# Where GpSimd widens the second norm's deviations in a two-direction state-space layer

## The chip, the cores and the metric

The kernel is one program on one core of a Trainium2 chip. The metric is the time of one execution on the device, in microseconds (us). Four runs of the kernel before took 17284.53 to 17308.42 us, with a median of 17295.28 us. A separate execution was recorded by the hardware profiler. It took 17300.45 us, and its span, from the first recorded instruction to the last, is 17298.6 us. All durations below are from that one execution.

A core has five engines with queues of their own: TensorE (PE in the profile, with PEld for its weight loads), VectorE (DVE), ScalarE (ACT), GpSimd (POOL) and SyncE (SP), which here only issues transfers. Each engine runs its queue in order, and an instruction at the head of a queue that waits holds up all behind it.

## The reference

The input is x, 8 images of 64 channels of 128 x 128 points, in float32. Four layers are applied one after the other, each as x = x + layer(groupnorm(x)): a deformable convolution, a 3x3 convolution, a pair of state-space scans, and a block that compares neighbouring points. The change lies in the third. Cut to what matters:

```python
def _layer_norm(x, g, b):                    # over the 64 channels of a point
    mu = jnp.mean(x, axis=-1, keepdims=True)
    var = jnp.mean((x - mu) ** 2, axis=-1, keepdims=True)
    return (x - mu) * jax.lax.rsqrt(var + EPS) * g + b
def _s5_block(x, i, ...):
    fx = _layer_norm(x, ln1_g[i], ln1_b[i])
    h = _s5_scan(fx, ...)                    # a scan forwards and one backwards
    x = jax.nn.gelu(h) + fx
    fx2 = _layer_norm(x, ln2_g[i], ln2_b[i]) # the second norm
    return fx2 @ ff_enc[i].T @ ff_dec[i].T + fx2
...
y_h = _s5_block(rows of the image, 0, *blk)
y_v = _s5_block(columns of the image, 1, *blk)
y = jnp.concatenate([y_h, y_v], axis=1)
return jnp.einsum('bihw,oi->bohw', y, fusion_w) + fusion_b[None, :, None, None]
```

Each of the two directions (rows, columns) has a forward and a backward scan over 16384 points. The second norm needs, for each point, one factor 1/sqrt(var + EPS), by which all 64 channels of that point are multiplied.

## The kernel before

The 8 images are handled as 4 pairs. The two images of a pair stand on the 128 partitions, 64 channels each. The deformable convolution of all pairs comes first, up to about 12100 us of the span. Then `rest` (line 451) takes pair after pair through the other three layers. In `scan_layer` (line 891) a pair first goes through `first_norm`, beside which the backward scan of direction 0 runs; then `ahead` (line 1250) runs for direction 0 with the backward scan of direction 1 beside it (the generator `aside`), and then `ahead` for direction 1 with nothing beside it.

`ahead` works in 16 groups of 1024 points (a group is 4 points by 256 blocks, and two images). A turn g of its loop is written in this order:

1. `scan(0, g + 1)`: the states of the next group (PE line 1154, ACT 1159, two DVE scans at line 1161).
2. `outputs(g)`: two PSUM tiles `py` from eight matmul calls (line 1208), gelu on ACT (1210), and the addition of `fx` on DVE (1211), into `h`, in two halves.
3. `rebuilt(g + 1)`: the states of the next group are turned back. For the backward and then the forward scan: a matmul `zt` (line 1187), a multiplication on GpSimd into `x` (1191), one on DVE into `xt` (1192) and a subtraction on GpSimd (1193). The tile `xt` has one buffer, so the second DVE multiplication needs the first subtraction to have read it.
4. `add(g - 1)`: for each half e of the group before: `spread` widens its 8 factors per partition to 8 x 64 on GpSimd (tile `yb`, line 849), four PE transposes bring them to channels in PSUM (`rb`, 852), ACT copies that to `rs` (1235), eight matmul calls mix the channels into `pm` (1240), DVE multiplies `pm` by `rs` (1241) and adds the result to the image in two instructions (1245). Tiles `yb` and `rs` have one buffer each. `rb`, `pm` and the tile `qc` below share one PSUM tag of two buffers.
5. `inputs(g + 2)` and `drive(g + 2)`: the drive of a later group, with one addition on GpSimd (`u`, line 1146).
6. `deviation(g)`: for each half a centring matmul (`qc`, 1220), a square on ACT (1222) and four small matmuls (1224) that leave 16 variances per partition; then `rsqrt` (line 104), 15 small DVE instructions in a row (`ln_...` in the profile, lines 108 to 118).
7. One step of `aside`: for direction 0 a turn of the backward scan of direction 1, with one more `u` on GpSimd.

This written order is not the order of the queues. The framework's planner goes over the instructions with costs of its own for each. When an engine is free in its reckoning, it takes from those that are ready then, with a free buffer for what they write, the one that was written first. So the written order decides only between instructions that are ready at the same time, and each engine's queue is what the planner's reckoning made of it. In the trace the order of GpSimd in a repeated turn of direction 0 is `u`, `u`, `yb` of half 0, both multiplications into `x`, the first subtraction, `yb` of half 1, the second subtraction.

`first_norm` (line 855) uses `spread` too, four times for each of its eight steps, with the tags `yb` and `xt` in turn.

Of the kernel before, what the change touches and what calls it, by code (L numbers as in the profile page):

```python
# [9 lines left out]
F32 = mybir.dt.float32  # L10
# [6 lines left out]
P = 128  # L17
C = 64
# [18 lines left out]
EPS = 1e-5  # L37
# [3 lines left out]
class Net:  # L41
# [800 lines left out]
            at = first + 2 * q  # L842
            self.nc.tensor.matmul(pv[:, at : at + 2], lhsT=sq[:, q * P : (q + 1) * P], rhs=self.imgmean, start=True, stop=True)  # L843

    def spread(self, wp, ptag, y, tag, ytag="yb"):

        nc = self.nc
        yb = wp.tile([P, 8, C], F32, tag=ytag, name=f"{tag}_yb", bufs=1)
        nc.gpsimd.tensor_copy(yb, y.unsqueeze(2).to_broadcast([P, 8, C]))  # L849
        rb = self.ps.tile([P, CH], F32, tag=ptag, name=f"{tag}_rb")  # L850
        for q in range(4):
            nc.tensor.transpose(rb[:, q * P : (q + 1) * P], yb[:, 2 * q : 2 * q + 2].rearrange("p i c -> p (i c)"), self.ident)
        return rb

    def first_norm(self, wp, p, a, b, r, nb):


        nc = self.nc
        af, bf = a.rearrange("p h w -> p (h w)"), b.rearrange("p h w -> p (h w)")
        center = wp.tile([P, P], F32, tag="center_r", name=f"center_r{p}", bufs=1)  # L860
        nc.vector.tensor_scalar(center, self.center, r, None, ALU.mult)
        pn = self.ps1.tile([P, 1], F32, tag="small", name=f"cn{p}")
        nc.tensor.matmul(pn, lhsT=self.center, rhs=nb, start=True, stop=True)
        cn = wp.tile([P, 1], F32, tag="cn", name=f"cns{p}", bufs=1)
        nc.vector.tensor_copy(cn, pn)

        def scale(n, y):
            for m in range(4):
                s = slice((4 * n + m) * CH, (4 * n + m + 1) * CH)
                rb = self.spread(wp, "y", y[:, 8 * m : 8 * m + 8], f"l1_{p}_{n}_{m}", ("yb", "xt")[m % 2])  # L870
                nc.vector.tensor_mul(bf[:, s], bf[:, s], rb)

        late = None
        for n in range(NCH // 4 - 1, -1, -1):
            pv = self.ps1.tile([P, 32], F32, tag="small", name=f"l1v{p}_{n}")
            for m in range(4):
                s = slice((4 * n + m) * CH, (4 * n + m + 1) * CH)
                pc = self.ps.tile([P, CH], F32, tag="x", name=f"pc{p}_{n}_{m}")
                nc.tensor.matmul(pc, lhsT=center, rhs=af[:, s], start=True, stop=True)
                sq = wp.tile([P, CH], F32, tag=("sq", "rs")[m % 2], name=f"sq{p}_{n}_{m}", bufs=1)  # L880
                nc.scalar.activation(sq, pc, AF.Square, bias=cn)
                nc.scalar.activation(bf[:, s], pc, AF.Identity, bias=cn)
                self.variances(pv, 8 * m, sq)
            if late:
                scale(*late)
                yield
            late = n, self.rsqrt(self.small, pv, 32, EPS, "ln32")
        scale(*late)
        yield

# [209 lines left out]
class Scan:  # L1100
# [112 lines left out]

    def deviation(self, g, hs):

        nc, net, tag = self.nc, self.net, f"{self.p}_{self.d}_{g}"
        pv = net.ps1.tile([P, 2, 2, 2, 2], F32, tag="small", name=f"l2v{tag}")
        for h in range(2):
            pc = net.ps.tile([P, CH], F32, tag="x", name=f"qc{tag}_{h}")
            nc.tensor.matmul(pc, lhsT=net.center, rhs=hs[:, h], start=True, stop=True)  # L1220
            sq = self.wp.tile([P, CH], F32, tag="sq", name=f"qs{tag}_{h}", bufs=1)
            nc.scalar.activation(sq, pc, AF.Square)
            for q in range(4):
                nc.tensor.matmul(pv[:, h, :, q % 2, q // 2], lhsT=sq[:, q * P : (q + 1) * P], rhs=net.imgmean, start=True, stop=True)
        return net.rsqrt(net.small, pv.rearrange("p a e m i -> p (a e m i)"), 16, EPS, "ln16")

    def add(self, g, hs, y):

        nc, net = self.nc, self.net
        for e in range(2):  # L1230
            h = hs[:, e]
            tag = f"{self.p}_{self.d}_{g}_{e}"
            rb = net.spread(self.wp, "x", y[:, 8 * e : 8 * e + 8], tag)
            rs = self.wp.tile([P, CH], F32, tag="rs", name=f"rs{tag}", bufs=1)
            nc.scalar.copy(rs, rb)
            pm = net.ps.tile([P, CH], F32, tag="x", name=f"pm{tag}")
            for j in range(2):
                mix = self.outs[:, MIX + j * C : MIX + (j + 1) * C]
                for i in range(2):
                    nc.tensor.matmul(pm[i * C : (i + 1) * C, j * NB : (j + 1) * NB], lhsT=mix, rhs=h[:, i, :], start=True, stop=True)  # L1240
            nc.vector.tensor_mul(rs, pm, rs)
            rs = rs.rearrange("p (j o m) -> p j o m", j=2, m=self.INNER)
            for j in range(2):
                at = self.blocks(self.a, g)[:, 2 * e + j]
                nc.vector.scalar_tensor_tensor(at, at, self.w["bias"], rs[:, j], ALU.add, ALU.add)  # L1245
        if self.d:
            for h in range(2):
                nc.vector.bn_stats(self.st[:, 2 * g + h, :], self.a[:, 64 * h : 64 * h + 64, 8 * g : 8 * g + 8])
# [70 lines left out]
```

## Time and profile before

| what | value |
|---|---|
| median of four runs | 17295.28 us |
| the profiled execution, its span | 17300.45 us, 17298.6 us |
| busy over the span: PE, DVE, POOL, ACT | 68%, 68%, 60%, 17% |
| a repeated turn of `ahead`, direction 0 (12580.00 to 12603.20 us) | 23.20 us: PE busy 21.83, DVE 16.34, ACT 9.65, POOL 9.54 |
| a repeated turn of `ahead`, direction 1 (13030.00 to 13050.55 us) | 20.55 us: PE busy 18.58, DVE 15.09, POOL 7.76, ACT 6.61 |
| granted PE clock in both turns | 1.00 |
| `yb` copies of `ahead`: instructions, one alone | 256, about 0.61 us |
| `yb` copies of `first_norm`: instructions, mean | 128, 615 ns |

Shares over the whole span are of little use here, since the layers have different limits. The change is read from the repeated turns, in the timeline, where each line gives the start in us, the duration, the engine, the line of the code, the instruction with its output and inputs, and in brackets how long the engine stood idle before it and what released it.

### The profile page before, as it was taken

The numbers are of one execution on the slowest core, as the hardware profiler recorded it, in microseconds if no ns is written. First come the engines' busy times: TensorE is split into PE (matmuls) and PEld (weight loads), VectorE is DVE, ScalarE is ACT, GpSimd is POOL, SyncE is SP. The second block draws the span as 40 slices with busy tenths as digits, with TensorE's granted clock in tenths as the row PEclk, the third lists the DMA queues.
The fourth block names the chain that finished last, engine by engine and source line by source line (L and its number), as shares of the span: only waits on it lengthen the run. The fifth ranks groups of instructions, "written<-read, shape, count | busy, mean of one in ns | idle before, by whom it ended". The sixth has DMA issues, their size and how long they took to land. (4 is left out here: it accounts for less than half of the span.)

```text
span 17298.6 us, 123578 instructions
## 1 busy us (share of the span) xinstructions
PE 11837.9 (68%) x33912; PEld 4220.1 (24%) x33912; DVE 11800.9 (68%) x27470; ACT 2925.7 (17%) x4956; POOL 10371.0 (60%) x10492
## 2 busy tenths in 40 slices
PE   5766565656675656666665665643898898898897
PEld 1111111111111111111111111111443443443443
DVE  5777777777777777777777777776465565565565
ACT  1101111111110011111001010001332332332331
POOL 3777777777777777777777777776232232232231
PEclk8977787877887768788787787865999999899897
DMA  6334444444433344443333333334223323323322
GB/s 192 121 116 127 140 149 151 133 147 143 146 117 115 114 134 146 148 134 116 113 116 114 114 117 113 113 107 138 52 57 97 94 55 101 90 56 101 92 53 73
DMA packets 966439, 1969.78 MB, mean 114 GB/s; under 512 B 216301, under 2 KB 517749, under 8 KB 931957
## 3 DMA queue, kind: packets, MB, share of 16 engines
q0 software_dynamic: 442368, 1208.55, 23.6%
q1 hardware_dynamic: 514532, 715.93, 13.4%
q10 hardware_dynamic: 8848, 37.40, 0.6%
q8 instruction: 275, 4.51, 0.1%
q14 instruction: 416, 3.40, 0.1%
HBM read 1516.67 MB, written 276.67 MB: 104 GB/s over the span
## 5 line engine op out<-in xcount | busy, mean ns | idle before, releaser
L388 POOL DMA_INDIRECT g<-table,idx x9216 | 8936.2, 970 | 2813.4 <-issue 2619.7
L397 DVE TENSOR_TENSOR g<-g,wts 128x256 f32<-128x256 f32 x9216 | 3805.3, 419 | 3138.0 <-DMA g<-table,idx 3123.2
L398 DVE TENSOR_REDUCE sm<-g 128x64 f32<-128x256 f32 x9216 | 4985.1, 579 | 0.9 <-DVE pos L352 0.2
L322 PE MATMUL po<-xe,wt 128*54 128x512 f32 (+3 forms) x8384 | 4730.1, 676 | 43.9 <-ACT ob L332 42.0
L402 PE MATMUL sp<-ident,sm 128*128 128x128 f32 x4096 | 1522.4, 376 | 4148.5 <-DVE sm L398 4136.4
L402 PEld LDWEIGHTS sp<-ident,sm 128*128 128x128 f32 x4096 | 625.6, 155 | 6930.9 <-DVE sm L398 5026.9
L405 ACT COPY s<-sp 128x512 f32<-128x512 f32 x1024 | 599.9, 586 | 8565.8 <-PE sp L402 8565.8
L322 PEld LDWEIGHTS po<-xe,wt 128*54 128x54 f32 x8384 | 929.6, 140 | 1415.4 <-issue 1068.0
L1146 POOL TENSOR_TENSOR u<-u,vs 128x512 f32<-128x512 f32 x256 | 326.0, 1274 | 1344.8 <-DVE vs L1145 1081.1
L411 PE MATMUL yp<-s,wd 128*64 128x512 f32 (+1 forms) x2560 | 823.5, 664 | 12.6 <-ACT s L405 12.6
L571 PE MATMUL c<-room,l_w 128*64 128x508 f32 (+1 forms) x3072 | 717.9, 597 | 16.0 <-DMA room<-nx 8.7
L849 POOL COPY l_yb<-ln_y 128x512 f32<-128x512 f32 x128 | 76.5, 615 | 1036.0 <-PE l1v L843 668.3
L1127 ACT ACTIVATE fx<-room,ln_b,ln_g 128x512 f32<-128x512 f32 x512 | 642.8, 1291 | 91.1 <-DMA in<-fx 61.7
L404 PE MATMUL s<-ident,sm 128*64 128x128 f32 x1024 | 346.7, 339 | 356.1 <-DVE sm L398 330.5
L1138 PE MATMUL pv<-in,tabs 128*128 128x512 f32 x1024 | 543.4, 654 | 5.2 <-DVE xt L1192 5.2
L1208 PE MATMUL py<-in,outs 128*128 128x512 f32 x1024 | 532.0, 624 | 2.7 <-ACT h L1210 2.7
L1208 PE MATMUL py<-x,outs 128*128 128x512 f32 x1024 | 504.0, 604 | 5.7 <-POOL x L1193 5.4
L1161 DVE TENSOR_TENSOR_SCAN z<-tabs,z,u 128x256 f32<-128x256 f32 x512 | 401.9, 804 | 82.1 <-POOL u L1146 59.6
L406 ACT COPY s<-s 64x128 f32<-64x128 f32 x1024 | 264.6, 258 | 722.7 <-PE s L404 722.2
L1245 DVE SCALAR_TENSOR_TENSOR room<-room,bias,rs 128x256 f32<-128x256 f32 x512 | 375.2, 785 | 6.9
L1193 POOL TENSOR_TENSOR x<-x,xt 128x512 f32<-128x512 f32 x256 | 327.8, 1281 | 68.0 <-DVE xt L1192 60.9
L1192 DVE TENSOR_TENSOR xt<-zt,tabs 128x512 f32<-128x512 f32 x256 | 175.6, 686 | 266.0 <-POOL x L1193 254.6
(1431 smaller groups left out, 11149.9 us busy)
## 6 DMA issues: line engine op xcount, KB each, us to landing
g<-table,idx POOLq DMA_INDIRECT x9216, 2.7
table<-q SPq DMA_DIRECT2D x512, 256.0 KB
in<-fx SPq DMA_DIRECT2D x1024, 128.0 KB
xe<-in_x_dram SPq DMA_DIRECT2D x56, 1408.0 KB
xs<-in_x_dram SPq DMA_DIRECT2D x32, 1024.0 KB
xt<-in_x_dram SPq DMA_DIRECT2D x32, 1024.0 KB
y<-ys SPq DMA_DIRECT2D x128, 256.0 KB
room<-in_x_dram SPq DMA_DIRECT2D x32, 1024.0 KB
```

Source lines behind the costliest of these rows:

```text
L322: nc.tensor.matmul(po[:, r0:r1, c0:c1], lhsT=wt[:, t, :], rhs=xe[:, row + r0 : row + r1, c0 + dx : c1 + dx], start=n == 0, stop=n == len(u ...
L388: nc.gpsimd.indirect_dma_start(out=tq[:, k, :], out_offset=None, in_=flat[i], in_offset=bass.IndirectOffsetOnAxis(ap=idx[:, at : at + 1], ...
L397: nc.vector.tensor_mul(t[:, k], t[:, k], w)
L398: nc.vector.tensor_reduce(sm[:, k], t[:, k].rearrange("p q c -> p c q"), axis=mybir.AxisListType.X, op=ALU.add)
L402: nc.tensor.transpose(sp[:, j, :], sm[:, j * P : (j + 1) * P], self.ident)
L405: nc.scalar.copy(st[i][:, 0:4, m * P : (m + 1) * P], sp)
L411: nc.tensor.matmul(yp[i * C : (i + 1) * C, :], lhsT=wd[0:rows, j, :], rhs=st[i][0:rows, j, :], start=j == 0, stop=j == 4)
L571: nc.tensor.matmul(o, lhsT=lt, rhs=mv, start=k < 2, stop=k >= len(calls) - 2)
L1127: nc.scalar.activation(fx[:, e].rearrange("p h (o m) -> p h o m", m=self.INNER), src[:, e::2], AF.Identity, bias=w["ln1_b"], scale=w["ln1_g"])
L1138: nc.tensor.matmul(pv, lhsT=tabs[:, at : at + P], rhs=fx[:, :, h, :], start=h == 0, stop=h == 1)
L1161: nc.vector.tensor_tensor_scan(z[:, i, 1 : NB + 1], tabs[:, DEC : DEC + 1].to_broadcast([P, NB]), u[:, i, :], z[:, i, 0:1], ALU.mult, ALU.add)
L1208: nc.tensor.matmul(py, lhsT=lt, rhs=mv, start=n == 0, stop=n == len(calls) - 1)
```

## The change

The widening on GpSimd is taken out of `spread` into a function `widen` of its own. In `ahead` it is now written at the end of `deviation(g)`, directly behind the `rsqrt` that makes the factors, for both halves, and with a buffer for each half (`yb0`, `yb1`) where there was one. `add` gets the widened tiles and starts with the transposes. In the written order the two copies of group g thus move from turn g + 1, behind `rebuilt(g + 2)`, to the end of turn g, ahead of the step of `aside` and of everything of turn g + 1. `first_norm` keeps its order and uses the tags `yb0` and `yb1` where it had `yb` and `xt`. The number of instructions of each kind stays, and no transfer is moved.

```diff
-    def spread(self, wp, ptag, y, tag, ytag="yb"):
+    def widen(self, wp, y, tag, ytag):
+
+        yb = wp.tile([P, 8, C], F32, tag=ytag, name=f"{tag}_yb", bufs=1)
+        self.nc.gpsimd.tensor_copy(yb, y.unsqueeze(2).to_broadcast([P, 8, C]))
+        return yb
+
+    def spread(self, ptag, yb, tag):
 
         nc = self.nc
-        yb = wp.tile([P, 8, C], F32, tag=ytag, name=f"{tag}_yb", bufs=1)
-        nc.gpsimd.tensor_copy(yb, y.unsqueeze(2).to_broadcast([P, 8, C]))
         rb = self.ps.tile([P, CH], F32, tag=ptag, name=f"{tag}_rb")
...
-                rb = self.spread(wp, "y", y[:, 8 * m : 8 * m + 8], f"l1_{p}_{n}_{m}", ("yb", "xt")[m % 2])
+                tag = f"l1_{p}_{n}_{m}"
+                rb = self.spread("y", self.widen(wp, y[:, 8 * m : 8 * m + 8], tag, ("yb0", "yb1")[m % 2]), tag)
...
-        return net.rsqrt(net.small, pv.rearrange("p a e m i -> p (a e m i)"), 16, EPS, "ln16")
-
-    def add(self, g, hs, y):
+        y = net.rsqrt(net.small, pv.rearrange("p a e m i -> p (a e m i)"), 16, EPS, "ln16")
+        return [net.widen(self.wp, y[:, 8 * h : 8 * h + 8], f"{tag}_{h}", f"yb{h}") for h in range(2)]
+
+    def add(self, g, hs, yb):
...
-            rb = net.spread(self.wp, "x", y[:, 8 * e : 8 * e + 8], tag)
+            rb = net.spread("x", yb[e], tag)
```

## The prediction

> **What bounds the kernel now.** I read the page first: over the span no engine is above 68%, but the slices show two halves, and the layer that the change touches lies in the second, where PE is at 80 to 90%. So the turns of that layer are the place. The windows of one repeated turn give PE 21.83 of 23.20 us (direction 0) and 18.58 of 20.55 (direction 1). PE thus stands still for 1.4 and 2.0 us a turn, and these are what a reordering on GpSimd can change. The timeline shows where. In direction 0:
>
> ```profile
> 12583.15 1.04 POOL L849 COPY 0_0_5_0_yb<-ln_y 128x512 f32<-128x512 f32 x1 [0.82 <-PE py L1208]
> 12584.15 1.27 POOL L1191 TENSOR_TENSOR x<-zb,tabs 128x512 f32<-128x512 f32 x1
> ...
> 12585.38 1.72 POOL L1191 TENSOR_TENSOR x<-z,tabs 128x512 f32<-128x512 f32 x1
> ...
> 12587.07 1.26 POOL L1193 TENSOR_TENSOR x<-x,xt 128x512 f32<-128x512 f32 x1
> 12588.28 0.60 POOL L849 COPY 0_0_5_1_yb<-ln_y 128x512 f32<-128x512 f32 x1
> 12588.36 0.69 DVE L1192 TENSOR_TENSOR xt<-zt,tabs 128x512 f32<-128x512 f32 x1 [1.79 <-POOL x L1193]
> 12588.97 0.68 DVE L1241 TENSOR_TENSOR rs<-pm,rs 128x512 f32<-128x512 f32 x1
> 12589.14 1.27 POOL L1193 TENSOR_TENSOR x<-x,xt 128x512 f32<-128x512 f32 x1 [0.25 <-DVE xt L1192]
> 12589.57 1.39 DVE L1161 TENSOR_TENSOR_SCAN z<-tabs,z,u 128x256 f32<-128x256 f32 x1
> ...
> 12592.21 0.59 ACT L1235 COPY rs<-0_0_5_1_rb 128x512 f32<-128x512 f32 x1 [4.52 <-DVE room L1245]
> 12592.84 0.30 PEld L1220 LDWEIGHTS qc<-h,center 128*128 128x128 f32 x2 [1.60 <-ACT rs L1235]
> ```
>
> See three things. GpSimd runs from 12583.15 to 12588.88 without a gap. DVE stands for 1.79 us for the first subtraction of that run, and behind its `xt` in the queue are `rs`, a scan and the two additions into the image. And the last wait before PE's `qc` comes from there: `qc` needs the buffer that ACT's copy `rs` frees, and that copy needs the additions. So the path is: `yb` of half 0, two multiplications, the subtraction, `xt`, `rs`, additions, ACT copy, `qc`, and then PE again. `yb` of half 1 is not on it: it fills the 0.7 us in which GpSimd would wait for `xt` anyway. Direction 1:
>
> ```profile
> 13012.49 0.94 POOL L849 COPY 0_1_8_0_yb<-ln_y 128x512 f32<-128x512 f32 x1 [0.79 <-DVE ln_y L118]
> 13013.39 1.27 POOL L1191 TENSOR_TENSOR x<-z,tabs 128x512 f32<-128x512 f32 x1
> 13014.62 1.27 POOL L1193 TENSOR_TENSOR x<-x,xt 128x512 f32<-128x512 f32 x1
> 13015.83 0.61 POOL L849 COPY 0_1_8_1_yb<-ln_y 128x512 f32<-128x512 f32 x1
> 13015.92 0.69 DVE L1192 TENSOR_TENSOR xt<-zt,tabs 128x512 f32<-128x512 f32 x1 [2.37 <-POOL x L1193]
> 13016.50 0.66 PE L852 MATMUL 0_1_8_1_rb<-ident,0_1_8_1_yb 128*128 128x128 f32 x4 [1.34 <-POOL 0_1_8_1_yb L849]
> 13019.08 0.59 ACT L1235 COPY rs<-0_1_8_1_rb 128x512 f32<-128x512 f32 x1 [1.55 <-DVE room L1245]
> 13019.71 0.19 PEld L1220 LDWEIGHTS qc<-h,center 128*128 128x128 f32 x1 [0.24 <-ACT rs L1235]
> ```
>
> Here PE does stand for `yb` of half 1, 1.34 us, but that wait ends on the same chain: `qc` is loaded at 13019.71, just behind ACT's copy (13019.67). The first multiplication ran before `yb` of half 0, at 13010.41.
>
> **The change, part by part.** The copies stay 256 in number and one kind; no transfer is issued by them, so SP's queue is untouched. In written order they pass, on POOL, the second `u` and the next turn's four rebuilding instructions.
>
> *Half 0's copy* waits for the last of the `rsqrt` instructions and starts within 0.2 to 0.3 us of it (`ln_y` ends at 12582.99, 13012.36). It can't start earlier. Behind it on POOL are only the rebuilding instructions, as now: 0.
>
> *Half 1's copy* now has its own buffer and no longer waits for the transposes of half 0. It is ready with half 0's and was written before the multiplications, so I place it right behind half 0's. It leaves a gap (0.61 us, free) and enters the path (0.61 us, paid).
> - Direction 0: first subtraction, `xt`, `rs`, additions and ACT copy shift by 0.61. The 0.48 us for which PE waits at the transposes of half 1 goes, and comes back in the wait at `qc`. What the copy displaces may change what meets what. The 1.72 us of the second multiplication beside `h` on DVE, against 1.27 alone, shows 0.45 of meeting. Lost: it costs 0.61 - 0.45 = 0.16; met once more: 0.61 + 0.45 = 1.06. I take 0.61, since the same two engines' work is still side by side. Turns with this order: groups 2 to 13, so 12 x 4 pairs = 48: 29 us (8 to 51).
> - Direction 1: ACT's copy ends at 13019.67 + 0.61 = 13020.28. PE, relieved of 1.34 us, has run dry by then. In direction 0 a `qc` found dry takes 1.12 us from its load, so it ends at about 13021.44 where it now ends at 13020.14 + 1.02 = 13021.16: +0.28. Groups 1 to 13, 52 turns: 15 us. Ends: 0 if PE's queue hides it, 0.61 x 52 = 32 us.
>
> On the meeting of GpSimd and DVE the Trainium skill has a rule (SBUF — State Buffer, Who interferes with whom): a DVE instruction with two SBUF inputs and a GpSimd instruction that reads SBUF exclude each other, and the one issued second waits for the first to end. The scan above, begun 0.43 us after a subtraction on GpSimd, took 1.39 us where scans alone take 0.74 to 0.76, so the row agrees in kind. By the rule `h` on DVE (ready at 12585.27) would wait for the multiplication that now runs from about 12584.8 to 12586.1, which pushes `xt` and adds some 0.3 us a turn, 14 us in all; the rule speaks against the change. I leave it outside the sum.
>
> *The turns at the ends* (groups 0, 1, 14, 15): in 14 and 15 the transposes of half 1 stand behind the mixing matmuls, which PE has to do anyway; at most 0.17 us of PE wait is seen for half 1's sake in group 14. In groups 0 and 1 one copy may save or cost 0.6. Ends: 16 turns x 0.61 = 10 us either way; I take 0.
>
> *`first_norm`*: two tags alternate as before, so its 128 copies keep order and waits: 0. The cover is the second buffer; with one, more would join the 211.3 us that these copies already wait for transposes, off the path. The 2 KB more of each partition cost no instruction: 0.
>
> Sum: 29 + 15 = +44 us. Against the profiled execution's 17300.45 that is 17344; the median stands 5 lower, so 17340. A measurement of this kernel tells about 0.2% (35 us) from no change, so this is just beyond it.
>
> **The rivals.**
> - *Hidden after all.* The planner's costs may make DVE's `rs` ready before the delayed `xt`. Then `rs` (0.68) moves out from behind `xt`, which pays for the 0.61: 0 in direction 0, and -0.3 to +0.28 in direction 1. In sum -16 to +15: about 17295. For it: in direction 0 PE's queue has other matmuls between the mixing and the transposes of half 1, so in the planner's reckoning half 1's copy ended after the mixing, and the delayed subtraction would too. Against: in direction 1 the transposes directly follow the mixing, so there the copy ended before it.
> - *Faster.* The same flip, but both additions (line 1245) pass `xt` too. The point from which it decides: `rs` and both additions stand before the second `xt` in DVE's queue. Then ACT's copy is free of GpSimd, and PE's waits for half 1's sake go: 0.48 of the 1.4 us and most of the wait at `qc`, some 1.0 a turn, in direction 0 (48 us), 1.34 in direction 1 (70). One direction alone gives 17240 to 17280, both about 17180. Against: DVE waits idle for `xt` now, and `xt` was written before them.
> - *Slower: the written order holds on POOL.* If both copies come before the first multiplication in direction 1 too, that multiplication (13010.41) waits for the `rsqrt`, and the subtraction ends at 13012.49 + 0.94 + 0.61 + 3 x 1.27 = 13017.85, not 13015.89: +2.0, less the 0.3 that PE hides, x 52 = 87, and with direction 0's 29 about 17410. Against: the multiplication is ready 2 us before the copy.
>
> **How the numbers follow.** As worked out: 0.40. Hidden: 0.20. Faster: 0.23. Slower: 0.17. The likeliest alone would be 17310 to 17380 (8 + 0 to 51 + 32, rounded in). The range leaves out the far half of the faster and the slower case: 17230 to 17400. Slower by over 0.2%: the rival's 0.17, 0.29 of the likeliest, 0.03 of the hidden: 0.49. Faster: 0.22 and 0.03: 0.25. Within: 0.26.
>
> **What would show it.** Right: in direction 0 POOL's order is two copies, two multiplications, two subtractions; the first subtraction starts 0.6 us later in the turn; PE waits no more at line 852 for half 1 but longer at 1220 for ACT's `rs`; turns of about 23.8 and 20.8 us. Wrong: DVE's line 1241 ahead of the second 1192, or a `yb` ahead of both multiplications in direction 1, or turns shorter than 23.2 and 20.5.

## The result and the profile after

The changed kernel took 17318.96 us (median of 40 runs), the kernel before 17295.56 us (median of 60 on the same chip). The ratio is 1.0013, with a 95% interval of 1.0008 to 1.0017: 23 us slower (14 to 29). That is a real difference, but below the 0.2% that the prediction set as its bound for a difference that one measurement tells. The profiled execution after has a span of 17312.1 us.

The timeline of the changed kernel, in the same turn of direction 0 as was shown of before (columns: start in us, duration, engine, line, instruction, and in brackets the idle time ahead of it with its releaser):

```profile
12592.58 1.06 POOL L848 COPY 0_0_5_0_yb<-ln_y 128x512 f32<-128x512 f32 x1 [0.79 <-DVE ln_y L118]
12593.58 0.61 POOL L848 COPY 0_0_5_1_yb<-ln_y 128x512 f32<-128x512 f32 x1
12594.16 1.27 POOL L1196 TENSOR_TENSOR x<-zb,tabs 128x512 f32<-128x512 f32 x1
12594.74 1.24 DVE L1216 TENSOR_TENSOR h<-h,in 128x512 f32<-128x512 f32 x1 [1.57 <-ACT h L1215]
12595.40 1.72 POOL L1196 TENSOR_TENSOR x<-z,tabs 128x512 f32<-128x512 f32 x1
12597.08 1.26 POOL L1198 TENSOR_TENSOR x<-x,xt 128x512 f32<-128x512 f32 x1
12598.38 0.69 DVE L1197 TENSOR_TENSOR xt<-zt,tabs 128x512 f32<-128x512 f32 x1 [1.79 <-POOL x L1198]
12598.98 0.68 DVE L1248 TENSOR_TENSOR rs<-pm,rs 128x512 f32<-128x512 f32 x1
12599.72 1.08 PE L1247 MATMUL pm<-h,outs 128*64 128x256 f32 x8 [1.42 <-DVE rs L1248]
12602.15 0.59 ACT L1242 COPY rs<-0_0_5_1_rb 128x512 f32<-128x512 f32 x1 [4.62 <-DVE room L1252]
12602.79 1.12 PE L1226 MATMUL qc<-h,center 128*128 128x512 f32 x2 [0.71 <-ACT rs L1242]
```

Half 1's copy stands right behind half 0's. Counted from the start of half 0's copy, the first subtraction now starts 4.50 us later, before 3.92; the second `xt` 5.80, before 5.21; `qc` 10.21, before 9.69. PE no longer waits at the transposes of half 1 (0.48 us in the turn shown of before). It waits twice further on: 1.42 us at `pm` of half 1, which is new, and 0.71 us at `qc`, where it stood 0.78 us before. In direction 1:

```profile
13029.43 1.01 POOL L848 COPY 0_1_8_0_yb<-ln_y 128x512 f32<-128x512 f32 x1 [0.72 <-DVE ln_y L118]
13030.38 0.61 POOL L848 COPY 0_1_8_1_yb<-ln_y 128x512 f32<-128x512 f32 x1
13030.96 1.27 POOL L1196 TENSOR_TENSOR x<-z,tabs 128x512 f32<-128x512 f32 x1
13032.18 1.27 POOL L1198 TENSOR_TENSOR x<-x,xt 128x512 f32<-128x512 f32 x1
13033.49 0.69 DVE L1197 TENSOR_TENSOR xt<-zt,tabs 128x512 f32<-128x512 f32 x1 [2.92 <-POOL x L1198]
13034.83 1.08 PE L1247 MATMUL pm<-h,outs 128*64 128x256 f32 x8 [1.00 <-DVE rs L1248]
13036.63 0.59 ACT L1242 COPY rs<-0_1_8_1_rb 128x512 f32<-128x512 f32 x1 [3.51 <-DVE room L1252]
13037.27 1.12 PE L1226 MATMUL qc<-h,center 128*128 128x512 f32 x2 [0.30 <-ACT rs L1242]
```

Only one of the two multiplications follows the copies here, so the other one still runs ahead of them. The 1.34 us for half 1's copy became 1.00 us at `pm` and 0.30 at `qc`.

The view of waits sums this over the run (columns: us in all, times, longest). Before:

```profile
PE qc L1220 <- ACT rs L1235: 36.7, 47, 1.4
...
PE pm L1240 <- DVE rs L1241: 2.0, 8, 0.4
```

After:

```profile
PE pm L1247 <- DVE rs L1248: 131.0, 108, 2.3
...
PE qc L1226 <- ACT rs L1242: 49.1, 98, 1.0
```

The transposes of half 1 have a line for each tile. Added up, PE waited there 42.1 us in direction 0 and 69.8 in direction 1 before, and nothing after. So 111.9 us of waits went, and 129.0 came at `pm` and 12.4 at `qc`: +29.5 us. The lengths of the stage say the same. I take the time of `ahead` from the start of the first widening copy of direction 0 (group 0) to that of the last group of direction 1 (group 15), added over the four pairs: 2756.9 us before, 2787.2 after, +30 us. The rest of the program differs by some tens of us between any two profiled executions (the time between the pairs, three gaps added, was 1770 to 1824 us in the fourteen profiles of this study); it is therefore left out of the sum.

### The profile page after: what moved, and what is told of

Same layout as the page of the kernel before. It is cut to its first block, busy times and chain, and to the rows that moved or that the text cites. A ratio compares the mean times of both kernels' runs of the same rounds, so it can differ in the third digit from the quotient of the medians.

```text
span 17312.1 us, 123466 instructions
## 1 busy us (share of the span) xinstructions
PE 11858.7 (68%) x33912; PEld 4206.4 (24%) x33912; DVE 11822.5 (68%) x27470; ACT 2924.0 (17%) x4956; POOL 10380.1 (60%) x10492
## 5 line engine op out<-in xcount | busy, mean ns | idle before, releaser
L411 PE MATMUL yp<-s,wd 128*64 128x512 f32 (+1 forms) x2560 | 815.8, 658 | 12.6 <-ACT s L405 12.4
L1247 PE MATMUL pm<-h,outs 128*64 128x256 f32 x2048 | 293.9, 404 | 131.0 <-DVE rs L1248 131.0
```

The costliest lines, as they stand in the source:

```text
L411: nc.tensor.matmul(yp[i * C : (i + 1) * C, :], lhsT=wd[0:rows, j, :], rhs=st[i][0:rows, j, :], start=j == 0, stop=j == 4)
```

## The experiments

The theory after the first look: what acts is the second buffer; it lets half 1's copy run early, which is no use to PE, because the same 0.61 us then delay the chain to PE's next matmul. The rivals: the written place acts; or the delay lies elsewhere than in that chain.

The table holds all runs. "Turn" is the mean distance of two copies of half 0, groups 3 to 13 in direction 0 and 2 to 13 in direction 1, and "stage" is the sum defined above, as a difference to before. All are from one profiled execution each. The ratio is that of the medians of the runs, against runs of the kernel before on the same chip. The four runs marked * were made on a chip on which the kernel before took 19353 us. The part ahead of the pairs is longer there. No profile of the kernel before was taken on it, but the stretch between the pairs takes the same time as on the other chips (1774 to 1824 us there, 1770 to 1823 on the others), and the turn of direction 1 is 20.56 us there in the kernel before with two `xt`, and 20.55 in the kernel before on another chip. So the turns of these runs are compared with the others, and their times only among themselves.

The mean of a turn hides one thing. In some turns the trace shows a granted TensorE clock of 0.5 for 3.41 or 6.83 us, and matmuls take up to twice as long there. The column "clock lowered" counts such turns, of 40 in direction 0 and 44 in direction 1, and "the rest" is the mean of the turns at a granted clock of 1.00 throughout, called undisturbed below.

| kernel | turn, dir. 0 | turn, dir. 1 | clock lowered | the rest | stage | ratio to before |
|---|---|---|---|---|---|---|
| before | 23.36 | 20.55 | 0, 0 | 23.36, 20.55 | 0 | 1 |
| after | 23.80 | 20.79 | 1, 0 | 23.76, 20.79 | +30 | 1.0013 [1.0008, 1.0017] |
| after, one buffer | 23.38 | 20.55 | 1, 0 | 23.34, 20.55 | -6 | 1.0005 [0.9996, 1.0014] |
| before, two buffers | 23.80 | 20.79 | 1, 0 | 23.76, 20.79 | +30 | 1.0018 [1.0009, 1.0027] |
| after, one copy more | 24.75 | 21.34 | 18, 0 | 24.35, 21.34 | +94 | 1.0048 [1.0034, 1.0061] |
| before, two `xt` * | 22.77 | 20.56 | 4, 0 | 22.45, 20.56 | -40 | 0.9959 [0.9945, 0.9972] |
| after, two `xt` | 22.55 | 19.64 | 0, 0 | 22.55, 19.64 | -111 | 0.9946 [0.9932, 0.9959] |
| before, two `rs` * | 22.34 | 20.66 | 1, 0 | 22.28, 20.66 | -44 | 0.9969 [0.9952, 0.9987] |
| after, two `rs` * | 22.86 | 20.81 | 2, 0 | 22.73, 20.81 | -12 | 1.0001 [0.9986, 1.0016] |
| after, two `xt`, two `rs` * | 21.36 | 19.58 | 0, 0 | 21.36, 19.58 | -178 | 0.9889 [0.9872, 0.9907] |
| after, ring | 23.59 | 22.34 | 0, 23 | 23.59, 21.02 | +61 | 1.0054 [1.0040, 1.0068] |
| before, two `rs`, ring | 23.83 | 20.46 | 6, 1 | 23.59, 20.43 | -37 | 0.9960 [0.9947, 0.9974] |
| after, two `rs`, ring | 22.80 | 20.47 | 3, 10 | 22.59, 20.12 | -96 | 0.9944 [0.9931, 0.9958] |
| after, two `xt`, two `rs`, ring | 21.38 | 18.39 | 0, 1 | 21.38, 18.34 | -269 | 0.9840 [0.9826, 0.9853] |

### Place or buffer

The change in place alone: written at the end of the turn, but with one buffer for both halves.

```diff
-        return [net.widen(self.wp, y[:, 8 * h : 8 * h + 8], f"{tag}_{h}", f"yb{h}") for h in range(2)]
+        return [net.widen(self.wp, y[:, 8 * h : 8 * h + 8], f"{tag}_{h}", "yb0") for h in range(2)]
```

> The place alone: both copies are written at the end of the turn as in the changed kernel, but the two halves share one buffer again. Theory (the second copy gets onto GpSimd's path because it has a buffer of its own): with one buffer it must wait for the transposes of half 0, so GpSimd's order and the turns are those of before (23.2 and 20.55 us), ratio 1.000 within 0.0007, about 17295 us. Rival (the written place does it): turns of 23.7 and 20.8 us as in the changed kernel, ratio 1.0013, about 17319 us.

The buffer alone, in the kernel before, where the copies stay written behind `rebuilt`:

```diff
-            rb = net.spread(self.wp, "x", y[:, 8 * e : 8 * e + 8], tag)
+            rb = net.spread(self.wp, "x", y[:, 8 * e : 8 * e + 8], tag, ("yb", "yb1")[e])
```

> The buffer alone: the kernel before, its copies written where they were, but each half with a buffer of its own in the second norm. Theory: the second copy is free to follow the first at once, so the whole loss is there: turns of 23.7 and 20.8 us, ratio 1.0013, about 17319 us. Rival (the written place does it): turns as before, ratio 1.000, about 17295 us.

With one buffer the turns are those of the kernel before, 23.38 and 20.55, and the ratio's interval includes 1. With the buffer alone they are those of the changed kernel to 0.01 us, and so is the stage. The timeline of the second kernel (before with two buffers), GpSimd:

```profile
12577.68 1.06 POOL L849 COPY 0_0_5_0_yb<-ln_y 128x512 f32<-128x512 f32 x1 [0.79 <-DVE ln_y L118]
12578.69 0.61 POOL L849 COPY 0_0_5_1_yb<-ln_y 128x512 f32<-128x512 f32 x1
12579.26 1.27 POOL L1191 TENSOR_TENSOR x<-zb,tabs 128x512 f32<-128x512 f32 x1
12580.49 1.72 POOL L1191 TENSOR_TENSOR x<-z,tabs 128x512 f32<-128x512 f32 x1
```

The copy of half 1 goes ahead of two multiplications that are written before it. So the move in the text, which is what the change is named for, does nothing by itself; the second buffer is the whole change.

### The price of GpSimd's time at this place

One more copy of half 1 into the same tile, directly behind the first; the output is the same.

```diff
-        return [net.widen(self.wp, y[:, 8 * h : 8 * h + 8], f"{tag}_{h}", f"yb{h}") for h in range(2)]
+        yb = [net.widen(self.wp, y[:, 8 * h : 8 * h + 8], f"{tag}_{h}", f"yb{h}") for h in range(2)]
+        nc.gpsimd.tensor_copy(yb[1], y[:, 8:16].unsqueeze(2).to_broadcast([P, 8, C]))
+        return yb
```

> The changed kernel with the copy of half 1 made twice, the second time into the same tile. Theory (GpSimd's queue ahead of the first subtraction is on the path of every repeated turn): one more 0.61 us in 48 turns of direction 0 and 52 of direction 1, some 60 us on top of the changed kernel: about 17380 us, ratio 1.0048, turns of 24.2 and 21.4 us. Rival (the loss is from what the copy meets on VectorE's side, or from the order alone, and GpSimd has room): no more than 15 us on top, ratio 1.001 to 1.002.

A turn grew by 0.95 us in direction 0 and by 0.55 in direction 1, so GpSimd's time is paid for at this place. The timeline of direction 0:

```profile
12561.65 1.06 POOL L848 COPY 0_0_5_0_yb<-ln_y 128x512 f32<-128x512 f32 x1 [0.80 <-DVE ln_y L118]
12562.66 0.61 POOL L848 COPY 0_0_5_1_yb<-ln_y 128x512 f32<-128x512 f32 x1
12563.33 0.61 POOL L1233 COPY 0_0_5_1_yb<-ln_y 128x512 f32<-128x512 f32 x1
...
12566.81 1.26 POOL L1198 TENSOR_TENSOR x<-x,xt 128x512 f32<-128x512 f32 x1
```

The first subtraction starts 5.16 us behind the first copy, 0.66 later than in the changed kernel. That the turn grew by more than the copy's 0.61 us has another cause: there are two sorts of turn. The windows of this turn and the next (columns: start and end, length, then busy time of PE, its weight loads, DVE, ACT, POOL, each with its instructions, the granted clock, the DMA share and GB/s):

```profile
12561.65:12586.66 25.01, 22.78 (x81) 11.23 (x80) 16.02 (x34) 9.45 (x15) 10.15 (x10) 0.93 0.25 64
12586.66:12611.00 24.34, 21.83 (x82) 10.64 (x81) 17.32 (x34) 9.89 (x15) 10.15 (x9) 1.00 0.25 65
```

In 18 of the 40 turns the granted clock was 0.5 for 3.4 us; they took 25.23 us in the mean, the undisturbed ones 24.35. Against the 23.76 us of the changed kernel's undisturbed turns the copy costs 0.59 us, close to its duration of 0.61. What lowered the clock was not tested. In direction 1 half 1's tile is finished later too, and 34.8 us of PE's waits are at the transposes of half 1 again, so there the price is not that of the late subtraction alone.

### Two buffers for `xt`

If the first subtraction no longer holds back the second `xt`, and with it `rs` and the additions in DVE's queue, then GpSimd's delay should not reach PE. In the kernel before this takes one more buffer:

```diff
-            t = wp.tile([P, 2, NB], F32, tag="xt", name=f"xt{f}{tag}", bufs=1)
+            t = wp.tile([P, 2, NB], F32, tag=("xt1", "xt")[f], name=f"xt{f}{tag}", bufs=1)
```

> The kernel before with a buffer of its own for each of the two tiles xt; half 1's copy stays in the single buffer yb and so behind the transposes of half 0. Theory A (the copy of half 1 is what PE then waits for): in direction 0 GpSimd's two subtractions no longer wait for DVE in turn, and the first xt can go before the multiplications end, so a turn loses about the 0.7 us by which the first subtraction held back rs and the additions: 48 x 0.7 = 34 us; in direction 1 PE stays bound by half 1's copy, 0. Ratio about 0.998. The pair with the changed kernel and two xt (0.9946) then says that the early copy of half 1 is worth some 60 us there, the opposite sign of what it does with one xt. Rival B (the second xt is worth the same whatever the copies do): ratio to before 0.9946 - 0.0013 or so, about 0.993 to 0.995, and the early copy is worth nothing with it.

In the changed kernel the same, with half 1's widened tile in the buffer of `sq`, since there is no room for one more (`first_norm` takes the tags `yb0` and `xt`):

```diff
-                rb = self.spread("y", self.widen(wp, y[:, 8 * m : 8 * m + 8], tag, ("yb0", "yb1")[m % 2]), tag)
+                rb = self.spread("y", self.widen(wp, y[:, 8 * m : 8 * m + 8], tag, ("yb0", "xt")[m % 2]), tag)
...
-            t = wp.tile([P, 2, NB], F32, tag="xt", name=f"xt{f}{tag}", bufs=1)
+            t = wp.tile([P, 2, NB], F32, tag=("xt1", "xt")[f], name=f"xt{f}{tag}", bufs=1)
...
-        return [net.widen(self.wp, y[:, 8 * h : 8 * h + 8], f"{tag}_{h}", f"yb{h}") for h in range(2)]
+        return [net.widen(self.wp, y[:, 8 * h : 8 * h + 8], f"{tag}_{h}", ("yb0", "sq")[h]) for h in range(2)]
```

> The changed kernel with two buffers for xt, so that VectorE's second multiplication no longer waits for GpSimd's first subtraction; to find the room, half 1's widened tile takes the buffer of the squares sq, which are read by then. Theory (the chain through the single xt is what makes the early copy cost, and without it PE's waits for half 1 are what is left): against the kernel before, direction 0 loses the waits at the transposes and at qc, some 1.2 us in 48 turns, direction 1 some 1.0 us in 52: 110 us faster, about 17185 us, ratio 0.9936, turns of about 22.0 and 19.6 us. Rival (the early copy costs by GpSimd's time as such, whatever VectorE waits for): within 15 us of the changed kernel, ratio 1.0005 to 1.002.

Both are faster than before, and the pair turns the sign of the change: with one `xt` the early copy costs 30 us of the stage, with two it saves 71 (-40 to -111). Of these, 41 us lie in the turns 2 to 13 of direction 1, where the kernel before with two `xt` still waits 69.8 us at the transposes of half 1. Direction 0 does not show this: its 9 us less come from four turns with a lowered clock in the kernel before with two `xt`, and the undisturbed turns are 22.45 us there and 22.55 in the changed kernel. The two ratios, from two chips, are too near to each other to show the worth of the copy. The kernel before with two `xt` has the turns of theory A (0.59 us less in direction 0, nothing in direction 1) but a lower ratio, 0.9959, than its 0.998. The changed kernel has the expected turn in direction 1, and 22.55 us instead of 22.0 in direction 0. It also keeps half 1's tile in the buffer of `sq`, which was not tested alone. The timeline of the changed kernel with two `xt`, and its view of waits:

```profile
12626.51 1.28 DVE L1197 TENSOR_TENSOR xt<-zt,tabs 128x512 f32<-128x512 f32 x2
...
12631.57 0.58 ACT L1242 COPY rs<-0_0_8_1_rb 128x512 f32<-128x512 f32 x1 [3.41 <-DVE room L1252]
```

```profile
PE qc L1226 <- ACT rs L1242: 58.2, 98, 1.6
```

Both `xt` now run in one piece, and the wait at `pm` is gone (4.1 us in all); PE's next wait is the one at `qc` for ACT's copy.

### Two buffers for `rs`

ACT's copy of half 1 then need not wait for the additions of half 0. In the kernel before with one more buffer, in the changed kernel with half 1's `rs` in the buffer `yb0`:

```diff
-            rs = self.wp.tile([P, CH], F32, tag="rs", name=f"rs{tag}", bufs=1)
+            rs = self.wp.tile([P, CH], F32, tag=("rs", "rs1")[e], name=f"rs{tag}", bufs=1)
```

> The kernel before with a second buffer for rs, so that ACT's copy of half 1 no longer waits for the additions of half 0. Theory A (the path to qc goes through that copy): the wait ahead of qc goes; direction 0 keeps 0.48 us of wait at the transposes of half 1, a turn of about 22.4 (-0.8 x 48 = -38 us); direction 1 keeps the 1.34 us at the transposes of half 1, whose release qc then follows, a turn of about 20.3 (-0.24 x 52 = -12 us). Ratio about 0.997. Rival B (the delay only moves on to the next user of the additions or of DVE): turns as before, ratio 1.000.

> The changed kernel with a second buffer for rs (half 1's rs in the buffer yb0, free by then). Theory A (the change's cost is only the longer chain to ACT's copy of rs, line 1242): with that wait gone the early copy is a gain: PE waits neither for half 1's copy nor at qc; turns of about 22.3 and 19.5 us, 48 x -1.4 and 52 x -1.2 against the changed kernel, ratio to the kernel before about 0.994; below the kernel before with two rs by 0.3%. Rival B (the later subtraction costs whatever happens to rs, since DVE's queue behind xt is late): the turns stay 0.4 and 0.2 longer than those of the kernel before with two rs.

And with two `xt` and two `rs` in the changed kernel:

> The changed kernel with two xt (as in the run that gave 0.9946) and two rs. Theory A: the 1.0 us of PE's wait for ACT's rs ahead of qc in direction 0 and the 0.2 us in direction 1 go: 48 + 10 = 58 us below the run with two xt, ratio to before about 0.991. Rival B: what PE waits for is then the next late thing (the copy of half 0 behind rsqrt, DVE's additions), and the ratio stays at 0.994.

The kernel before came out as expected of theory A in direction 0 (22.34), where `qc` did wait for ACT; direction 1 did not gain (20.66, where 20.3 was expected); it still waits 69.6 us for half 1's copy. The changed kernel went the rival's way: its turns stay 0.52 and 0.15 us longer, and the early copy still costs 32 us of the stage (-44 to -12). The timeline of the changed kernel with two `rs`, and its view of waits:

```profile
14649.00 0.68 DVE L1248 TENSOR_TENSOR rs<-pm,rs 128x512 f32<-128x512 f32 x1
...
14649.74 1.08 PE L1247 MATMUL pm<-h,outs 128*64 128x256 f32 x8 [1.41 <-DVE rs L1248]
```

```profile
PE pm L1247 <- DVE rs L1248: 128.9, 109, 2.2
```

So the delay does not need ACT's copy to reach PE. `rb`, `pm` and `qc` share two accumulators in turn, and `pm` of half 1 takes the one that `pm` of half 0 holds until DVE's `rs` has read it. That is the nearer way back, and here the theory of the prediction fell. With two `xt` as well, which brings `rs` forward, the stage fell by 67 us (-111 to -178) where theory A had 58; nearly all of it came in direction 0, 1.20 us a turn (1.0 expected), and 0.06 in direction 1 (0.2 expected).

### The ring of accumulators

Half 1's product is put into the ring of `py` instead.

```diff
-            pm = net.ps.tile([P, CH], F32, tag="x", name=f"pm{tag}")
+            pm = net.ps.tile([P, CH], F32, tag="xy"[e], name=f"pm{tag}")
```

> The changed kernel with half 1's product pm in the other accumulator ring (tag y instead of x), so that its matmuls need not wait until DVE's rs has read half 0's product. Theory C, formed from the last runs (the change's cost returns at two places, at pm through that ring, 131 us of PE's wait, and at qc through ACT's single rs): the wait at pm goes, and since ACT's copy of half 1 still waits for the additions, most of it comes back at qc: turns between those of the changed kernel and 0.3 us less, ratio to before 0.999 to 1.002. Theory A of the prediction (the path goes through ACT's rs alone): turns unchanged, 23.7 and 20.8, ratio 1.001.

> The changed kernel with both ways back open: two buffers for rs, and half 1's product in the other ring. Theory C: nothing that PE needs waits for the late subtraction any more; the 129 us of waits at pm and the 23 at qc go, less some 0.4 us a turn that qc then waits for rs of half 0: turns of about 21.9 and 20.1 us, ratio to before about 0.994, although the subtractions and xt still start 0.6 us late in the turn. Rival D (DVE and GpSimd are late as such, and the delay reaches the next turn some other way, by rsqrt or the state update): turns of 22.7 and 20.8 as with two rs alone, ratio 1.000.

> The kernel before with the same two rs and the same ring for half 1's product, half 1's copy late as ever. Theory C: PE is bound by the transposes of half 1, which wait for that copy, so the ring brings nothing: turns of about 22.3 and 20.6 as with two rs alone, ratio 0.997. The pair with the run above then gives the worth of the early copy with both ways open: -0.4 and -0.5 us a turn, some 45 us less time, where it is 23 us more in the kernel as it stands. Rival D: the pair stays as it was with two rs alone, the early copy 0.5 and 0.15 us a turn dearer.

> The fastest so far (two xt, two rs, early copy: turns of 21.3 and 19.6) with half 1's product in the other ring. Theory C: with two xt the product of half 0 is read early and PE waits only 4.7 us there, so the ring brings nothing: turns 21.2 to 21.4 and 19.5 to 19.6, ratio to before 0.989 to 0.992. Rival D: no different number.

The wait at `pm` went to nothing in all four, but theory C's ratios missed in the first and the last, and of the turns only some came as expected. In the changed kernel alone the time rose to 1.0054. There the wait moved to `qc`, which now takes half 0's accumulator, while ACT still waits for the additions. Its timeline and its view of waits:

```profile
12576.13 1.13 PE L1226 MATMUL qc<-h,center 128*128 128x512 f32 x2 [1.64 <-DVE rs L1248]
12577.91 0.59 ACT L1242 COPY rs<-0_0_5_1_rb 128x512 f32<-128x512 f32 x1 [5.41 <-DVE room L1252]
```

```profile
PE qc L1226 <- DVE rs L1248: 156.3, 100, 1.9
```

The longer time does not come from this wait: PE's waits at `pm` and `qc` for an `rs` were 180.1 us in the changed kernel. It comes from the granted clock. In 23 of the 44 turns of direction 1 it was 0.5 for 6.8 us, and these turns took 23.55 us, the others 21.02. Two that follow each other (columns as above):

```profile
12952.30:12973.32 21.02, 18.46 (x74) 9.42 (x73) 14.30 (x31) 6.32 (x10) 7.83 (x7) 1.00 0.13 39
12973.32:12996.81 23.49, 21.73 (x74) 10.94 (x73) 14.26 (x31) 6.41 (x10) 7.82 (x7) 0.85 0.12 33
```

PE is idle for less of the longer turn (1.76 us, not 2.56) but busy for 3.27 us more. The 23 turns cost 58 us together, more than the 31 us by which the stage exceeds that of the changed kernel. Why the clock fell here was not tested.

With two `rs` the wait at `qc` is the same, 154.3 us:

```profile
PE qc L1226 <- DVE rs L1248: 154.3, 100, 2.0
```

so this kernel did not open the way that I meant to open; its ratio of 0.9944 hits the expected number although that wait stayed. The planner also made other queues of it: on GpSimd an addition `u` moved in between the copies and the multiplications, and on PE both `qc` come in one run. Its partner, the kernel before with the same two edits, waits longer still for half 1's copy:

```profile
12580.56 0.66 PE L852 MATMUL 0_0_5_1_rb<-ident,0_0_5_1_yb 128*128 128x128 f32 x4 [1.88 <-POOL 0_0_5_1_yb L849]
...
13007.97 0.66 PE L852 MATMUL 0_1_8_1_rb<-ident,0_1_8_1_yb 128*128 128x128 f32 x4 [2.06 <-POOL 0_1_8_1_yb L849]
```

Added up it is 96.7 and 111.3 us. So in this pair the early copy exchanges 206 us of waits (2 are left) for 154, and the stage is 59 us shorter (-37 to -96). Theory C had the sign and 45 us, but by waits that vanish and not by an exchange.

The last kernel, with two `xt`, two `rs` and the ring, is the fastest, against the expectation that the ring would bring nothing: 16992.66 us, 1.6% below before. In direction 0 the ring did bring nothing (21.36 and 21.38 us); the gain is in direction 1 (19.58 and 18.39). The windows (columns as above), first a turn of direction 1 without the ring, then one of each direction with it:

```profile
15009.46:15029.05 19.59, 18.63 (x73) 9.24 (x72) 15.78 (x32) 6.53 (x10) 8.08 (x8) 1.00 0.16 42
```

```profile
12560.60:12581.83 21.23, 21.23 (x81) 10.64 (x80) 15.97 (x34) 9.59 (x14) 9.75 (x9) 1.00 0.29 75
12949.88:12968.17 18.29, 18.29 (x74) 9.44 (x73) 15.48 (x31) 6.40 (x10) 8.05 (x7) 1.00 0.16 44
```

PE is busy for the whole of both turns with the ring. In direction 1 without it PE still waited 0.82 us at the transposes of half 0, for the copy behind the `rsqrt`; with it the last variances are ready 11.5 us into the turn instead of 12.9.

## Why the prediction was right, and where it was not

The predicted time was 17340 us with a range of 17230 to 17400; measured were 17318.96, 0.13% above before. The sign is that of the likeliest case, the size half of it, and it belongs to the class "within 0.2%", to which the prediction gave 0.26 and not its highest chance.

- *Half 0's copy, 0.* Right: it still follows `ln_y`, and POOL stood 0.79 and 0.72 us ahead of it, before 0.82 and 0.79. (From the prediction's own numbers it starts 0.16 and 0.13 us behind the end of `ln_y`, not 0.2 to 0.3.)
- *Half 1's copy right behind half 0's.* Right in both directions, but one of its two reasons was idle. "Was written before the multiplications" plays no part, as the kernel with the buffer alone shows; "its own buffer" is enough.
- *Direction 0, 0.61 us a turn.* The middle case between the two meetings came true: the second multiplication took 1.72 us again. The subtraction came 0.58 us later. ACT's copy came 0.51 later, and the shown turn grew from 23.20 to 23.67, 0.47. So two small pieces of the delay, 0.07 behind the `rs` and 0.04 behind ACT's copy, were taken up. On the mean of all turns it was 0.44, 21 us in 48 turns and not 29. That the mean turn of 23.80 us meets the forecast of 23.8 is luck: the forecast adds 0.61 to the shown turn of 23.20, and the mean before was 23.36.
- *Direction 1, 0.28 us a turn.* 0.25, 13 us in 52 turns and not 15. `qc` found dry took 1.12 us, as was assumed.
- *The ends, 0.* Within the stated 10 us: the stage as a whole grew by 30, where these means would give 34.
- *The sum, 44.* The mis-sized term is direction 0's, 29 us where 21 were measured. Between the stage's 30 and the runs' 23 (14 to 29) there is no difference that a single profile could tell.
- *The way back to PE.* This step failed in part. The prediction has PE's wait "come back in the wait at `qc`", by way of the additions and ACT's copy. 12 us came back there; 129 came at `pm` of half 1, through the accumulator that waits for DVE's `rs`. The price came out nearly right because both ways begin with the same late `rs`; the forecast made from it, that two `rs` would turn the change into a gain, was wrong. The trace of before had this way in it, and the prediction, which followed the chain from `qc` back, passed over it. There the weight load for `pm` of half 1 was already released by that `rs`, which ended at 12589.65, 0.05 us behind the transposes:

```profile
12589.70 0.63 PEld L1240 LDWEIGHTS pm<-h,outs 128*64 128x64 f32 x8 [0.35 <-DVE rs L1241]
```

- *The rivals.* On DVE `rs` stays behind the second `xt` in the changed kernel, so neither "hidden after all" nor "faster" came about. The condition of "slower" did not occur either: the first multiplication of direction 1 still runs ahead of the copies.
- *The skill's rule* (the Trainium skill, SBUF — State Buffer, Who interferes with whom). By it `h` on DVE would wait for the multiplication on GpSimd. The trace agrees in kind: `h` started at 12594.74 beside the multiplication that began at 12594.16 and ended at 12595.43, and took 1.24 us where it took 0.70 before. It ended 0.55 us behind the multiplication, 0.15 earlier than a full wait and 0.70 us would give. Its mean over the layer rose from 744 to 822 ns. The 0.3 us a turn that the prediction worked out from the rule, 14 us, did not reach the path: the first subtraction starts right behind the second multiplication, at 12597.08, and not behind `xt`, which was done at 12596.59. Leaving it outside the sum was right.

The general account that holds in all four pairs is one of exchange: the early copy takes away PE's waits for half 1's transposes and pays with PE's waits for the late `rs`.

| pair | waits that went | waits that came | stage, after minus before |
|---|---|---|---|
| as they stand | 111.9 | 141.4 | +30 |
| two `rs` | 111.4 | 139.1 | +32 |
| two `xt` | 129.1 | 54.1 | -71 |
| two `rs`, ring | 205.8 | 154.3 | -59 |

The waits that went are the fall of PE's waits at the transposes of half 1; those that came are the rise of its waits at `pm` and `qc` for an `rs` of DVE or ACT. In all four rows the two account for the stage to within 8 us. The account is one of PE's waits alone: it leaves out turns lengthened by a lowered clock, and the rise from the changed kernel to the same with the ring does not follow from it.

## What to carry to other kernels

A buffer that lets an operation run early does not make it free: ask what the engine would have done in that time, and who waits for that. Here 0.61 us on GpSimd moved from a gap to the head of a chain, and the same edit changed from a loss of 30 us of the stage to a gain of 71 once the chain behind it was loosened with one more buffer. Where a planner makes the queues, look first at which buffers an edit gives and takes; and when following a delay to the engine that bounds the time, list every ring of buffers that it can come back through, not only the one that ends last in the trace of before. And look at the granted clock of single turns before a longer turn is put down to a wait.

## What the runs showed of the hardware

On one of the chips the kernel before took 19353 us instead of 17268 to 17296, at a mean granted clock of 0.77 instead of 0.83. Nearly the whole difference lies ahead of the pairs: the first widening copy of the layer started at 14475 to 14529 us there and at 12433 to 12467 on the others, while the time between the pairs does not differ (1774 to 1824 us and 1770 to 1823). Why the first part is longer there is open.

In the repeated turns the granted clock was 1.00 but for stretches of 0.5 that last 3.41 or 6.83 us. In the kernel with one more copy the matmul calls of `pm` took 1.85 us in such a stretch, where they take 1.08, and those of `py` 1.77 instead of 1.10. How many turns had one depended on the kernel, from none of 84 before to 23 in the changed kernel with the ring.
